# First pass over attention scores: masks added by VectorE with the maximum, or by TensorE products

## Chip, cores and metric

The kernel runs on one core of a Trainium2 chip. The metric is the device time of one execution in microseconds (us). Before the change it is 1712.83 us, the median of three runs (1712.34 to 1717.03).

## What is computed

Two layers on 2048 tokens of width 512, each an attention and a feed-forward part beside each other. The change lies in the attention of the second layer: 16 heads of width 32, causal, with a window of 1024 tokens back:

```python
q = rmsnorm(q, q_gamma); k = rmsnorm(k, k_gamma)
q = q * cos + rotate_half(q) * sin
k = k * cos + rotate_half(k) * sin
mask = (q_idx >= k_idx) & (q_idx - k_idx <= WINDOW)
scores = einsum('bhqd,bhkd->bhqk', q, k) / sqrt(HD)
scores = where(mask, scores, NEG)          # NEG = -1e30
attn = softmax(scores, axis=-1)
out = einsum('bhqk,bhkd->bhqd', attn, v)
```

The feed-forward part of the second layer chooses 256 of the tokens, and runs a small attention (heads of width 128) and a gated multilayer part on them alone.

## The kernel before, in words

**Two passes over the scores.** The kernel first makes all scores only to find the maximum of each query and head. A later stage makes them again, transposed, with the negated maxima added in a product, and takes the exponential. The first pass is `maxima` (L616). It works on one row of 128 queries at a time (i = 0 to 15), and in a row on groups g of four heads. A row sees the causal blocks of 128 keys back to the window, at most nine (NWB, L30); these are split in up to three chunks of at most four blocks. A chunk of one group is one *step*: a row has 4 steps in rows 0 to 3, 8 in rows 4 to 7, 12 in rows 8 to 15, 144 in all.

A step does the following. Four products of 32 contraction rows (one for each head, side by side in the array) write the scores into tile `pa` in PSUM, [128, 4, 512] (L633). Where a chunk holds the diagonal block (`last`) or, from row 8 on, the block at the window's edge (`edge`), four more products add a mask block: the identity times a mask of zeros and -1e30 in bf16 (L639, L641). No chunk holds both in its own blocks: where there is an edge there are three chunks, and 96 of the 144 steps have one mask. Then one VectorE reduction over all four heads writes the maxima of the chunk to `mx` (L645). `pa` has one buffer (pool `ps_a`, bufs=1, L719)[...]. At a row's end four small reductions (L649 to L653) turn the maxima into two bf16 parts of the negated maximum, four transposes (L658, tile `tn`) turn them, and ScalarE copies them to `negT`.

**What runs beside it.** The steps are cut up by a generator and spread by class `Steps` (L663): `some(below, weight)` adds a rate to a debt, and issues a step whenever the debt reaches one. Up to about row 7 the steps stand between the projections of the second layer (L965, 12 products of 512 columns for each token tile), the transposes (L110), and the routing that picks the 256 tokens. For each tile VectorE sums squares (L755), takes a reciprocal (L79), scales q and k (L758) and copies transposed k (L114); POOL rotates q and k (L763 to L773). Afterwards they stand between the feed-forward part's products: projections (L1042), its small attention (L1122, L1159), the output projection (L1175), gate and up (L1210, L1214), down (L1225). VectorE adds biases (L1047), masks and reduces scores (L1126, L1132) and multiplies (L1218) there. `late.rest()` (L1230) issues what is left. The second pass (L1285 on) begins with its first product at L1296, once `pa` has given its PSUM back.

**What sets the order.** Each engine works through its own queue in order. The source gives a priority, not the order itself: the tile framework schedules all instructions of the program when it is built, and may move an instruction past others of its engine. So the order in a queue can change where only an instruction's kind changes. Waits between engines, and of an engine on itself, are semaphores that the framework places.

Of the kernel before, what the change touches and what calls it, by code (L numbers as in the profile page):

```python
# [19 lines left out]
P = 128  # L20
# [18 lines left out]
def two_layer_kernel(ctx: ExitStack, tc: tile.TileContext, a: dict, out: bass.AP):  # L39
# [529 lines left out]
    G.tensor_copy(ident_b, ident)  # L569


    mask = const([P, 3, P], "mask", l1)
    maskT = const([P, 2, P], "maskT", l1)
    maskT_b = const([P, 2, P], "maskT_b", l1, BF16)
    mask_b = const([P, 3, P], "mask_b", l1, BF16)
    for m in (mask, maskT):
        G.memset(m, 0.0)
    for m, step, mult in (
        (mask[:, 0, :], 1, -1), (mask[:, 2, :], -1, 1), (maskT[:, 0, :], -1, 1), (maskT[:, 1, :], 1, -1)
    ):  # L580
        G.affine_select(
            out=m, in_=m, pattern=[[step, P]], compare_op=ALU.is_ge, fill=NEG, base=0,
            channel_multiplier=mult,
        )
    G.tensor_copy(mask_b, mask)
    G.tensor_copy(maskT_b, maskT)
    ones_b = const([P, P], "ones_b", l1, BF16)
    G.memset(ones_b, 1.0)
# [27 lines left out]
    def maxima(i, ps_a):  # L616


        nb = min(i + 1, NWB)
        kb0 = i + 1 - nb  # L620
        nch = -(-nb // 4)
        mx, nm, pn = mxs[i % 2], nms[i % 2], parts[i % 2]
        for g in range(NC):
            lo = 0
            for c in range(nch):
                w = nb // nch + (c < nb % nch)
                ks = slice((kb0 + lo) * P, (kb0 + lo + w) * P)
                edge = nb == NWB and c == 0
                last = c == nch - 1
                pS = ps_a.tile([P, 4, 4 * P], F32, tag="a", name=f"pa_{i}_{g}_{c}")  # L630
                for h in range(4):
                    r = slice(h * HD, (h + 1) * HD)
                    PE.matmul(  # L633
                        pS[:, h, : w * P], qT[r, g, i * P : (i + 1) * P], kT[r, g, ks],
                        start=True, stop=not (edge or last),
                    )
                for h in range(4):
                    if edge:
                        PE.matmul(pS[:, h, 0:P], ident_b, mask_b[:, 0, :], start=False, stop=True)  # L639
                    if last:  # L640
                        PE.matmul(  # L641
                            pS[:, h, (w - 1) * P : w * P], ident_b, mask_b[:, 2, :],
                            start=False, stop=True,
                        )
                V.tensor_reduce(mx[:, g, :, c], pS[:, :, : w * P], AX.X, ALU.max)  # L645
                yield
                lo += w

        V.tensor_reduce(nm[:, :, :, 0], mx[:, :, :, :nch], AX.X, ALU.max, negate=True)  # L649
        V.tensor_reduce(pn[:, :, :, 0], nm[:, :, :, 0:1], AX.X, ALU.max)  # L650
        V.tensor_reduce(nm[:, :, :, 1], pn[:, :, :, 0:1], AX.X, ALU.max, negate=True)
        with nc.allow_low_precision(reason="the low part of a split in two"):
            V.tensor_reduce(pn[:, :, :, 1], nm, AX.X, ALU.add)  # L653

        def turn(pool, tag):
            tn = pool.tile([P, NC, P], BF16, tag=tag, name=f"tn_{i}")
            for g in range(NC):
                PE.transpose(tn[:, g, :], pn[:, g].rearrange("p h d -> p (h d)"), ident_b)  # L658
            scopy(negT[:, :, i * P : (i + 1) * P], tn)

        yield turn
# [335 lines left out]
    with ExitStack() as p5:  # L997
# [110 lines left out]
        def attend(ch, q2T):  # L1108


            rep = NH2 // NKV2
            probs = []
            for j in range(2):
                n = (j + 1) * P
                nm = f"{ch}_{j}"
                pr = wk.tile([P, NHC, K2], F32, tag="pr", name=f"pr_{nm}")
                mx = wk.tile([P, 2, NHC], F32, tag="mx2", name=f"mx2_{nm}")
                for h0 in range(0, NHC, 2):
                    pS = ps.tile([P, 2, K2], F32, tag="mm", name=f"s2_{nm}_{h0}")
                    for hh in range(2):  # L1120
                        h = h0 + hh
                        PE.matmul(  # L1122
                            pS[:, hh, :n], q2T[:, h, j * P : (j + 1) * P],
                            k2T[:, (ch * NHC + h) // rep, 0:n], start=True, stop=True,
                        )
                    V.scalar_tensor_tensor(  # L1126
                        pr[:, h0 : h0 + 2, :n], pS[:, :, :n], 1.0 / math.sqrt(HD2),
                        mask[:, 2 - j : 3, :].rearrange("p b k -> p (b k)").unsqueeze(1)
                        .to_broadcast([P, 2, n]), ALU.mult, ALU.add,
                    )  # L1130
                late.some(weight=0.9 * (j + 1))
                V.tensor_reduce(mx[:, 0, :], pr[:, :, :n], AX.X, ALU.max, negate=True)  # L1132
                for hl in range(NHC):
                    S.activation(
                        pr[:, hl, :n], pr[:, hl, :n], AF.Exp, bias=mx[:, 0, hl : hl + 1],
                        accum_out=mx[:, 1, hl : hl + 1],
                    )
                V.reciprocal(mx[:, 1, :], mx[:, 1, :])
                for hl in range(NHC):
                    S.activation(  # L1140
                        pr[:, hl, :n], pr[:, hl, :n], AF.Copy, scale=mx[:, 1, hl : hl + 1]
                    )
                probs.append(pr)
            yield
            for j in range(2):
                nm = f"{ch}_{j}"
                pT = []
                for b in range(j + 1):
                    pT.append(wk.tile([P, NHC, P], F32, tag="pT", name=f"pT_{nm}_{b}"))
                    transpose4(  # L1150
                        ps, lambda c: probs[j][:, c, b * P : (b + 1) * P], pT[b],
                        f"trp_{nm}_{b}", scopy, tag="mm",
                    )
                late.some(weight=0.5 * (j + 1))
                po = ps.tile([P, NHC, P], F32, tag="mm", name=f"o2_{nm}")
                for h0 in range(0, NHC, rep):
                    kvh = (ch * NHC + h0) // rep
                    for b in range(j + 1):
                        PE.matmul(  # L1159
                            po[:, h0 : h0 + rep, :].rearrange("p h q -> p (h q)"),  # L1160
                            v2[:, b, kvh * HD2 : (kvh + 1) * HD2],
                            pT[b][:, h0 : h0 + rep, :].rearrange("p h q -> p (h q)"),
                            start=b == 0, stop=b == j,
                        )
                late.some(weight=0.9 * (j + 1))
                vcopy(oT[:, ch * NHC : (ch + 1) * NHC, j * P : (j + 1) * P], po)
            yield
# [336 lines left out]
```

## Time and profile before

| what | value |
|---|---|
| median of 3 runs | 1712.83 us |
| the profiled execution, its own time | 1715.47 us |
| its span | 1713.8 us |
| granted TensorE clock, mean | 0.994 |
| first and last score block of the first pass (start) | 747.8 and 1328.1 us |
| reductions L645 | 144, 252.9 us; 0.69, 1.22, 1.76, 2.29 us for one to four blocks |
| mask products L639 and L641 | 128 and 256, 12.7 and 25.6 us of records |

The page of the profile lists one execution. A group line gives source line, engine, operation, output and inputs with their shapes, and the number of instructions; then the busy time and the mean of one in ns; then the idle time of the engine in front of them, and what ended most of it. A record of a matrix product lasts longer than its share of the engine, since products overlap in the array: the spacing of starts tells what one costs. A product of fp32 data is two records. "PEld" is the loading of weights, which overlaps the products.

### The profile page before, as it was taken

Reading aid. Unit: us, or ns where it says so; the run is one execution under the profiler, and the core shown is the slowest. Engines: PE = TensorE matmul, PEld = TensorE weight load, DVE = VectorE, ACT = ScalarE, POOL = GpSimd, SP = SyncE. Lnnn points to the kernel's source line nnn. Section 1 sums busy time; section 2 is a strip of 40 time slices with the busy share of each in tenths; the row PEclk is TensorE's granted clock in tenths of the full one; section 3 lists DMA queues with packets and bytes.
Section 4 is the critical chain, followed back from the end, with each engine's and each line's share of the span. In section 5 each row is a group of like instructions: output and inputs, shape, how many; then the busy total and the mean of one; then the engine's idle time right before and its main releaser. Section 6 shows DMA issues by size and latency. Waiting matters only on the chain.

```text
span 1713.8 us, 20410 instructions
## 1 busy us (share of the span) xinstructions
PE 1657.4 (97%) x8114; PEld 743.6 (43%) x8114; DVE 982.5 (57%) x1256; ACT 588.2 (34%) x939; POOL 500.0 (29%) x398
## 2 busy tenths in 40 slices
PE   8999999999999999989999989899999999999999
PEld 3445444444444444444443434454564333333343
DVE  4754746345445543357566676675555477557565
ACT  3213333243253344221111110431100566447473
POOL 3230000000000200053574423330000677558584
PEclk9999999999999999999999999999899999999999
DMA  9411001120030431111010034112232300110101
GB/s 360 169 37 47 25 25 37 47 88 25 25 111 25 94 104 50 62 56 56 25 32 26 28 118 153 62 50 74 74 99 74 99 1 2 50 50 2 50 1 38
DMA packets 62384, 109.23 MB, mean 64 GB/s; under 512 B 12528, under 2 KB 14064, under 8 KB 61520
## 3 DMA queue, kind: packets, MB, share of 16 engines
q1 hardware_dynamic: 55856, 106.12, 18.7%
q0 software_dynamic: 1152, 1.21, 0.4%
q10 hardware_dynamic: 5280, 0.59, 0.3%
q8 instruction: 63, 1.03, 0.3%
q14 instruction: 33, 0.27, 0.1%
HBM read 86.24 MB, written 21.67 MB: 63 GB/s over the span
## 4 chain that ended last, share of the span: by engine, by line
PE 81%; DVE 10%; ACT 2%; DMA 2%; POOL 2%; issue 2%; SPq 0%; DVEq 0%; POOLq 0%; ACTq 0%
PE ea L494 6%; PE acc L478 6%; PE eg L492 6%; PE ps L1296 6%; PE pa L633 6%; PE p L965 6%; PE av L1370 5%; PE po L553 3%; PE pq L367 3%; PE po L1340 3%; PE gx L242 3%; DVE mx L645 3%; PE mg L1210 2%; PE pao L1175 2%; PE pm L1225 2%; PE po L555 2%
## 5 line engine op out<-in xcount | busy, mean ns | idle before, releaser
L645 DVE TENSOR_REDUCE mx<-pa 128x4 f32<-128x1536 f32 (+3 forms) x144 | 252.9, 1756 | 151.2 <-PE pa L641 72.2
L1403 POOL TENSOR_TENSOR acc<-acc,pt 128x1024 f32<-128x1024 f32 (+2 forms) x110 | 252.9, 2328 | 96.6 <-DVE acc L1403 43.4
L1330 ACT ACTIVATE pt<-ps 128x1024 f32<-128x1024 f32 (+3 forms) x208 | 181.4, 924 | 108.1 <-PE ps L1319 61.5
L1403 DVE TENSOR_TENSOR acc<-acc,pt 128x1024 f32<-128x1024 f32 (+1 forms) x80 | 144.4, 1832 | 103.9 <-POOL acc L1403 103.9
L633 PE MATMUL pa<-kT,qT 32*128 32x384 f32 (+3 forms) x1152 | 139.8, 541 | 19.8 <-DVE mx L645 16.1
L350 ACT ACTIVATE r_e<-eg 128x512 f32<-128x512 f32 x128 | 75.9, 594 | 201.6 <-PE eg L492 194.4
L1296 PE MATMUL ps<-qT,kT 32*128 32x512 f32 (+3 forms) x1152 | 139.9, 524 | 0.0
L352 DVE TENSOR_TENSOR h<-ea,r_e 128x512 f32<-128x512 f32 x128 | 87.2, 685 | 84.5 <-ACT r_e L351 83.5
L743 POOL TENSOR_TENSOR cosg<-cosg,gam 128x512 f32<-128x512 f32 x2 | 2.5, 1264 | 442.7 <-DVE gam L740 442.7
L492 PE MATMUL eg<-xl,rwgT 128*128 128x512 f32 x256 | 130.7, 592 | 0.0
L494 PE MATMUL ea<-xw,rw1T 128*128 128x512 f32 x256 | 130.7, 592 | 0.0
L478 PE MATMUL acc<-h,rw2T 128*128 128x512 f32 x256 | 129.2, 592 | 0.0
L965 PE MATMUL p<-w_qk,xnt 128*128 128x512 f32 x256 | 123.2, 604 | 2.3 <-DVE qk L758 2.3
L1370 PE MATMUL av<-pt,v 128*32 128x512 f32 (+3 forms) x1024 | 100.8, 482 | 0.0
L1296 PEld LDWEIGHTS ps<-qT,kT 32*128 32x128 f32 x1152 | 54.7, 183 | 94.7 <-issue 65.8
L633 PEld LDWEIGHTS pa<-kT,qT 32*128 32x128 f32 x1152 | 46.8, 185 | 103.3 <-DVE mx L645 64.9
L488 DVE TENSOR_TENSOR xw<-xw,xl 128x512 f32<-128x512 f32 x64 | 43.8, 685 | 83.5 <-DMA xw<-w_d 83.2
L351 ACT ACTIVATE r_e<-r_e 128x512 f32<-128x512 f32 x128 | 80.3, 629 | 5.7 <-ACT r_e L350 1.9
L478 PEld LDWEIGHTS acc<-h,rw2T 128*128 128x128 f32 x256 | 48.6, 190 | 61.3 <-issue 52.1
L492 PEld LDWEIGHTS eg<-xl,rwgT 128*128 128x128 f32 x256 | 48.6, 190 | 61.2 <-issue 61.0
L494 PEld LDWEIGHTS ea<-xw,rw1T 128*128 128x128 f32 x256 | 48.6, 190 | 61.2 <-issue 59.3
L288 PE MATMUL pk<-k_wT,xnT 128*128 128x512 f32 x128 | 61.3, 622 | 3.5 <-ACT xnT L117 3.5
(336 smaller groups left out, 2420.0 us busy)
## 6 DMA issues: line engine op xcount, KB each, us to landing
xw<-w_d SPq DMA_DIRECT2D x64, 256.0 KB, 3.2
x<-in_x SPq DMA_DIRECT2D x16, 256.0 KB, 4.7
res_d<-x SPq DMA_DIRECT2D x16, 256.0 KB, 2.1
xr<-res_d SPq DMA_DIRECT2D x16, 256.0 KB, 4.2
xn_d<-xn SPq DMA_DIRECT2D x16, 256.0 KB, 3.0
res_d<-xr SPq DMA_DIRECT2D x16, 256.0 KB, 3.1
xnq<-xn_d SPq DMA_DIRECT2D x16, 256.0 KB, 2.8
v_d<-vt SPq DMA_DIRECT2D x16, 256.0 KB, 2.0
```

The source lines that it names most:

```text
L351: S.activation(r, r, AF.Square)
L352: V.tensor_tensor(dst, pa, r, ALU.mult)
L478: PE.matmul(acc, rw2T[:, j, e, :], h, start=e == 0 and j == 0, stop=e == E - 1 and j == 1,)
L492: PE.matmul(pg, rwgT[:, e, hb], xl, start=True, stop=True)
L494: PE.matmul(pa, rw1T[:, e, hb], xw, start=True, stop=True)
L633: PE.matmul(pS[:, h, : w * P], qT[r, g, i * P : (i + 1) * P], kT[r, g, ks], start=True, stop=not (edge or last),)
L645: V.tensor_reduce(mx[:, g, :, c], pS[:, :, : w * P], AX.X, ALU.max)
L965: PE.matmul(pj, xnt[:, c, :], w, start=c == 0, stop=c == NC - 1)
L1296: PE.matmul(pS[h // 2][:, h % 2, t0 * P - q0 : (t1 + 1) * P - q0], kT[r, g, kb * P : (kb + 1) * P], qT[r, g, t0 * P : (t1 + 1) * P], start ...
L1330: S.activation(pT[:, :, :n], pS[hp][:, :, :n], AF.Exp)
L1370: PE.matmul(self.av[h * HD : (h + 1) * HD, t0 * P - o : (t1 + 1) * P - o], vs[kb // 4][:, kb % 4, hs], got[h // 2][:, h % 2, t0 * P - q0 : ...
L1403: eng.tensor_tensor(part, part, got[hp][:, :, : q1 - q0], ALU.add)
```

## The change

VectorE now adds the masks. `mask` gets five blocks in place of three (edge, three of zeros, diagonal), so that a slice of it fits every masked chunk, with the mask at its first or its last block. In a masked step the mask products are gone. The one reduction is replaced by four `tensor_tensor_reduce`, one for each head: each adds the mask slice to the scores in place in PSUM, and takes the maximum of the sums into one column of `mx`. In the built program each is two instructions, the operation and a read of its accumulator. Steps without a mask keep the reduction. The bf16 copy `mask_b` is gone, and the other user of `mask` (L1126) takes its slice from the new places.

```diff
--- before.py
+++ after.py
@@ -569,20 +569,18 @@
     G.tensor_copy(ident_b, ident)
 
 
-    mask = const([P, 3, P], "mask", l1)
+    mask = const([P, 5, P], "mask", l1)
     maskT = const([P, 2, P], "maskT", l1)
     maskT_b = const([P, 2, P], "maskT_b", l1, BF16)
-    mask_b = const([P, 3, P], "mask_b", l1, BF16)
     for m in (mask, maskT):
         G.memset(m, 0.0)
     for m, step, mult in (
-        (mask[:, 0, :], 1, -1), (mask[:, 2, :], -1, 1), (maskT[:, 0, :], -1, 1), (maskT[:, 1, :], 1, -1)
+        (mask[:, 0, :], 1, -1), (mask[:, 4, :], -1, 1), (maskT[:, 0, :], -1, 1), (maskT[:, 1, :], 1, -1)
     ):
         G.affine_select(
             out=m, in_=m, pattern=[[step, P]], compare_op=ALU.is_ge, fill=NEG, base=0,
             channel_multiplier=mult,
         )
-    G.tensor_copy(mask_b, mask)
     G.tensor_copy(maskT_b, maskT)
     ones_b = const([P, P], "ones_b", l1, BF16)
     G.memset(ones_b, 1.0)
@@ -632,17 +630,19 @@
                     r = slice(h * HD, (h + 1) * HD)
                     PE.matmul(
                         pS[:, h, : w * P], qT[r, g, i * P : (i + 1) * P], kT[r, g, ks],
-                        start=True, stop=not (edge or last),
+                        start=True, stop=True,
                     )
-                for h in range(4):
-                    if edge:
-                        PE.matmul(pS[:, h, 0:P], ident_b, mask_b[:, 0, :], start=False, stop=True)
-                    if last:
-                        PE.matmul(
-                            pS[:, h, (w - 1) * P : w * P], ident_b, mask_b[:, 2, :],
-                            start=False, stop=True,
+                if edge or last:
+
+                    m = mask[:, 0:w, :] if edge else mask[:, 5 - w : 5, :]
+                    m = m.rearrange("p b k -> p (b k)")
+                    for h in range(4):
+                        s = pS[:, h, : w * P]
+                        V.tensor_tensor_reduce(
+                            s, s, m, 1.0, LOW, ALU.add, ALU.max, accum_out=mx[:, g, h, c : c + 1]
                         )
-                V.tensor_reduce(mx[:, g, :, c], pS[:, :, : w * P], AX.X, ALU.max)
+                else:
+                    V.tensor_reduce(mx[:, g, :, c], pS[:, :, : w * P], AX.X, ALU.max)
                 yield
                 lo += w
 
@@ -1125,7 +1125,7 @@
                         )
                     V.scalar_tensor_tensor(
                         pr[:, h0 : h0 + 2, :n], pS[:, :, :n], 1.0 / math.sqrt(HD2),
-                        mask[:, 2 - j : 3, :].rearrange("p b k -> p (b k)").unsqueeze(1)
+                        mask[:, 4 - j : 5, :].rearrange("p b k -> p (b k)").unsqueeze(1)
                         .to_broadcast([P, 2, n]), ALU.mult, ALU.add,
                     )
                 late.some(weight=0.9 * (j + 1))
```

## The prediction

> **What bounds the kernel now.** The page first: its engine line says that TensorE is nearly full over the whole span, and group L645 that VectorE's maxima wait for TensorE, while TensorE's scores (L633) wait for the maxima.
>
> ```profile
> PE 1657.4 (97%) x8114; PEld 743.6 (43%) x8114; DVE 982.5 (57%) x1256; ACT 588.2 (34%) x939; POOL 500.0 (29%) x398
> ```
> ```profile
> L645 DVE TENSOR_REDUCE mx<-pa 128x4 f32<-128x1536 f32 (+3 forms) x144 | 252.9, 1756 | 151.2 <-PE pa L641 72.2
> L633 PE MATMUL pa<-kT,qT 32*128 32x384 f32 (+3 forms) x1152 | 139.8, 541 | 19.8 <-DVE mx L645 16.1
> ```
>
> Second the windows view, for the two halves of the stage where tile pa lives (query rows 0 to 7, then 8 to 15). Columns: PE, PEld, DVE, ACT, POOL busy.
>
> ```profile
> 748.00:957.00 209.00, 194.21 (x964) 86.55 (x960) 140.76 (x157) 38.70 (x75) 111.21 (x112) 0.99 0.12 32
> 957.00:1331.00 374.00, 353.47 (x1888) 184.01 (x1888) 232.72 (x237) 71.06 (x181) 69.89 (x89) 0.98 0.25 83
> ```
>
> PE is 94% busy in this stage (547.7 of 583), DVE 64%. TensorE is the bound, but thinly: third, the timeline of one exchange.
>
> ```profile
> 1243.77 0.93 PE L633 MATMUL pa<-kT,qT 32*128 32x384 f32 x8
> ...
> 1244.62 0.40 PE L639 MATMUL pa<-mask_b,ident_b 128*128 128x128 bf16 x4
> ...
> 1245.06 1.76 DVE L645 TENSOR_REDUCE mx<-pa 128x4 f32<-128x1536 f32 x1 [0.69 <-PE pa L639]
> 1245.08 1.95 PE L1210 MATMUL mg<-hT_b,wg 128*128 128x256 f32 x8
> ...
> 1246.96 0.93 PE L633 MATMUL pa<-kT,qT 32*128 32x384 f32 x8
> ...
> 1247.95 1.76 DVE L645 TENSOR_REDUCE mx<-pa 128x4 f32<-128x1536 f32 x1 [1.14 <-PE pa L633]
> ```
>
> There is one buffer of pa. Scores and masks fill it, the maximum empties it, and only then may the next scores start. So each step lasts as long as the longer of two things: TensorE's own work between two score blocks (here 0.85 scores, 0.24 masks, 0.22 for tn, 1.75 for mg), and the **loop** through pa. The loop of a masked step of three blocks is 1.29 from scores to maximum, 1.76 for it, and 0.05 or more back: 3.10, which is also the shortest spacing of such maxima (967.06 to 970.16 in the timeline). Unmasked: 0.99 + 1.76 + 0.05 = 2.80. The work in between is only a little longer.
>
> **The change, part by part.** Of 144 steps 96 are masked: 4 of one block, 8 of two, 76 of three, 8 of four.
>
> *Removed on PE*: 384 mask products. The timeline starts one every 0.056 us (four take 0.23), so 384 x 0.056 = about 22 us, all on the engine that bounds the stage.
>
> *Added on DVE*: 384 add-and-max instructions and 384 accumulator reads for 96 reductions. No row shows this instruction. The nearest, in the groups by form, read scores in PSUM with the mask in SBUF, and accumulate:
>
> ```profile
> L98 DVE SCALAR_TENSOR_TENSOR sj<-xn,wr 128x512 f32<-128x512 f32 x16 | 10.9, 684 | 0.1
> L1126 DVE SCALAR_TENSOR_TENSOR pr<-s,mask 128x512 f32<-128x512 f32 x8 | 5.3, 678 | 0.0
> L1126 DVE SCALAR_TENSOR_TENSOR pr<-s,mask 128x256 f32<-128x256 f32 x8 | 3.2, 419 | 4.7 <-PE s L1122 4.7
> L98 DVE DVE_READ_ACCUMULATOR sj<-xn,wr 128x1 f32 x16 | 1.3, 81 | 0.0
> ```
>
> On the line through 678 and 419 a head of three blocks takes 0.548, its accumulator read 0.08. In the built program every such instruction waits for the one before it on its own engine; rows that do so (L649 to L653) stand 0.04 apart. So 0.67 a head, 2.68 a step against 1.756: +0.92. For one, two and four blocks it is 1.61 against 0.69, 2.16 against 1.22, 3.19 against 2.29. Over 96 steps that is +88 us on DVE, to some 462 us of a stage of 600.
>
> Bounds. The low end: the page "VectorE: DVE Perf Modes" of the Trainium skill, section "Rules for kernel authors", tells one not to fuse chained operations for speed but to lower their count; here one becomes eight. Its errata section prices an operation from PSUM at 120 cycles plus one per element, at 0.96 GHz. By that four heads take 4 x 0.525 = 2.10 us; it gives no price for the accumulator read or the wait between, which the rows do: 2.68. My sum below is +11 us by the page and +20 by the rows; I take the rows. The high end, 0.8 a head: L332, another such operation from PSUM, takes 0.341 for 128 columns where the line gives 0.29, and writing back into PSUM may add as much again; sum +40. Two cycles per element I exclude, since both L98 (accumulating) and L645 take 1.04 ns per element.
>
> *The loop then*: a masked step of three blocks is 0.99 + 2.68 + 0.05 = 3.72 against 3.10: +0.62. The first add-and-max waits for all four heads' scores, so nothing of it starts sooner.
>
> *What moves.* Since the program is scheduled as it is built, the order of PE's instructions changes too. Comparing both built orders: masked steps get more other work behind them (4.4 us in place of 3.7 in many), which would cover 3.72; but the work of a row isn't more than before, so the end of a row has none. In rows 7 to 14 the last score block is followed directly by the next row's:
>
> ```
> before: pa_3_1  mu x3 mg x4  pa_3_2  mu x4   pa_0_0 (row 15)  tn  mg x4
> after:  pa_3_1  mu x4        pa_3_2          pa_0_0 (row 15)  tn  mg x4  mu x2
> ```
>
> There TensorE has 0.94 us of work in a loop of 3.72 (2.8 us idle); there are 13 such empty steps, and 9 more are short by over 0.3 us.
>
> I added up the larger of work and loop for all 144 steps in both orders. A 512-column f32 product counts two records of 0.43 us, 256 columns half, a 128-column transpose 2 x 0.11, and score blocks 0.43, 0.64, 0.85, 1.06 for one to four blocks; 0.09 for the load before a score block. In us:
>
> | rows | work before | larger, before | work after | larger, after |
> |---|---|---|---|---|
> | 0-3 | 71.5 | 71.5 | 73.0 | 73.0 |
> | 4-7 | 129.6 | 129.6 | 127.7 | 136.6 |
> | 8-11 | 177.6 | 178.8 | 163.5 | 187.5 |
> | 12-15 | 175.8 | 178.4 | 168.5 | 181.7 |
> | all | 554.5 | 558.3 | 532.7 | 578.8 |
>
> So 22 us of products go, TensorE's idle time in these loops grows from 4 to 46, and the balance is **+20.5 us**. With the old order and the new loop the sum is only +3. The trace has 580.2 from the first to the last score block, 22 above the sheet: other VectorE work in front of a maximum, a weight load at 1014 (5 us). I keep these 22 as they are.
>
> *Queued behind*: the changed DVE order puts 25 us of other operations (copies of kT, qk, act, biases) between the heads of masked steps, where they lengthen the loop. 22 of the 96 masked steps have no cover, so 25 x 22/96 = **+6 us**. Those operations themselves wait up to 2 us longer for heads in front of them; POOL's rotation waits for qk (62.9 us already), with a tile of time to spare.
>
> *At nothing*: the longer memset and the dropped cast on POOL (418 and 502 ns at 587 us) fall in a stage where POOL sits idle; uncovered they would gain a few tenths of a us. No DMA moves across another. From the first L1296 on, the orders of both programs are the same on every engine, so the last 383 us stay.
>
> Sum: 1715.5 (span 1713.8 and 1.7 around it) + 26 = 1742. The profiled execution is 2.6 above the median of 1712.8, so 1739.
>
> **Rivals.**
> - *Faster: the cover holds.* TensorE stays the bound in every step and the longer loop hides behind products, as 94% busy suggests; then only the 22 us go: 1691. Place: the 22 short steps at the ends of rows; they would have to find work. It decides at some 0.33 us a head: below that the sheet turns negative even with the new order, and no row is near. Chance 0.08.
> - *Balance.* Rows cheaper than the page and little interleaving: within 5 us (0.3%, about what a measurement can tell from none): 1713. Chance 0.08.
> - *VectorE becomes the bound.* In row 8, DVE has 8 x 2.68 + 4 x 1.76 of maxima, about 12 us of other work (3.6 for each of three token tiles: rr 1.22, its reciprocal 0.35, qk 2 x 0.69, kT 0.68; and the row's end), and must stand off for 12 x 1.0 us of scores: 52 us against 48 in the sheet. If the other work never fits, all 25 us land, or a head costs 0.8: +45 to +60, say 1765. For it: row 8 took 48.0 us before by the timeline, where its work in the sheet is 45.2. Against: much of that work fits while scores are made. Chance 0.27.
> - *Forecast*, 1722 to 1755: chance 0.57.
>
> The range leaves out the faster case, part of balance, and the upper end of the third: 1716 to 1778. Faster by over 0.3% 0.08, same 0.08, slower 0.84.
>
> **What would show it.** 384 add-and-max rows of 0.55 us for three blocks with 384 reads of 0.08, and DVE up by 88 us; 4 heads in 2.7 us; PE's waits for pa from 16 to over 40 us, most at ends of rows, two score blocks 3.7 apart with nothing between; the stage after unchanged in length. I am wrong if a head takes under 0.4 or over 0.8 us, if PE's idle time isn't at the ends of rows, or if the qk and POOL chain opens a wait of its own.

## The result, and the profile after

The changed kernel takes 1779.35 us (median of 4 runs, 1775.04 to 1779.95) against 1713.57 for the kernel before (4 runs): a ratio of 1.0375, 95% interval 1.0352 to 1.0398, **65.8 us slower**. The forecast was 1739, in a range that ended at 1778. The sign was right, the size less than half.

From the page of the changed kernel: the engines; the granted clock in 40 slices; the two groups that now take the place of the one maximum, and the scores.

```profile
PE 1669.2 (94%) x7730; PEld 738.2 (42%) x7730; DVE 1047.8 (59%) x1928; ACT 588.8 (33%) x939; POOL 499.6 (28%) x397
...
PEclk9999999999999999999998869899899899999999
...
L641 DVE CUSTOM_DVE_ANT_0 pa<-pa,mask 128x384 f32<-128x384 f32 (+3 forms) x384 | 212.5, 553 | 106.8 <-PE pa L631 97.8
...
L631 PE MATMUL pa<-kT,qT 32*128 32x384 f32 (+3 forms) x1152 | 148.9, 586 | 62.0 <-DVE mx L641 44.2
...
L645 DVE TENSOR_REDUCE mx<-pa 128x4 f32<-128x1536 f32 (+1 forms) x48 | 88.5, 1844 | 61.1 <-PE pa L631 60.9
```

Two things to see. TensorE now waits 62.0 us in front of score products (19.8 before). And although 384 mask products are gone, TensorE's busy time *grew*, by 11.8 us: its products became slower. The PEclk row says why: 8s and a 6 in the slices of the score stage, where before had a single 8:

```profile
PEclk9999999999999999999999999999899999999999
```

The timeline shows both in one place, the end of row 14 (start, us, engine):

```profile
1341.20 0.93 PE L631 MATMUL pa<-kT,qT 32*128 32x384 f32 x8
1344.85 0.93 PE L631 MATMUL pa<-kT,qT 32*128 32x384 f32 x8 [2.73 <-DVE mx L641]
1345.82 0.52 PE L658 MATMUL tn<-ident_b,parts 128*128 128x128 bf16 x4
1346.13 3.55 PE L1210 MATMUL mg<-hT_b,wg 128*128 128x256 f32 x8
```

Two score blocks stand 3.65 us apart with nothing between: the empty step of the prediction, called *bare* from here on. Then the same eight products mg that took 1.95 us in the kernel before take 3.55. The trace's clock record has half the clock from 1345.96 for 3.41 us. All stretches of half clock in this record last 3.41 us or a multiple of it, but for one that the end of the execution cuts short.

The windows view of one stretch (PE, PEld, DVE, ACT, POOL busy, then the granted clock) of the kernel after, and of the kernel before:

```profile
1021.00:1056.00 35.00, 20.03 (x84) 8.62 (x85) 21.22 (x58) 3.29 (x8) 0.00 (x0) 0.51 0.28 100
```
```profile
1021.00:1056.00 35.00, 35.00 (x176) 15.15 (x176) 22.47 (x20) 2.93 (x5) 16.58 (x24) 1.00 0.60 214
```

These are the ends of rows 7 and 8 in the changed kernel: 34 us on end at a clock of 0.51, TensorE busy for 57% of it.

**An account of the stage.** I cut each trace at the first score block and at the first product of the last stage (L1296 after), and measured in between: how long some TensorE record runs ("covered"), the rest ("idle"), how long the granted clock is at half, and TensorE's covered time in those stretches. A product takes about twice as long there (those of mg start 0.427 us apart, and 0.216 at full clock), so half of that covered time is my estimate of what the clock costs.

| kernel | time, us | ratio to before, 95% | stage | covered | idle | at half clock | covered at half |
|---|---|---|---|---|---|---|---|
| before | 1713.57 | 1 | 587.5 | 552.2 | 35.2 | 17.1 | 16.1 |
| after | 1779.35 | 1.0375 (1.0352 to 1.0398) | 648.8 | 561.6 | 87.2 | 116.1 | 83.8 |
| no_masks | 1701.98 | 0.9923 (0.9897 to 0.9949) | 574.3 | 539.7 | 34.6 | 34.1 | 31.2 |
| add_then_max | 1781.76 | 1.0380 (1.0355 to 1.0406) | 653.9 | 563.2 | 90.6 | 122.8 | 88.4 |
| both | 1795.89 | 1.0465 (1.0440 to 1.0490) | 667.3 | 579.7 | 87.6 | 109.2 | 80.0 |
| fill | 1757.36 | 1.0245 (1.0221 to 1.0270) | 631.4 | 567.2 | 64.2 | 61.4 | 45.7 |
| warm | 1785.41 | 1.0443 (1.0415 to 1.0470) | 653.7 | 566.2 | 87.5 | 92.2 | 69.1 |
| warm2 | 1762.81 | 1.0286 (1.0269 to 1.0303) | 635.1 | 562.8 | 72.3 | 64.9 | 55.9 |
| new_order | 1776.14 | 1.0366 (1.0349 to 1.0384) | 651.0 | 579.4 | 71.6 | 102.4 | 78.3 |
| old_order | 1753.17 | 1.0234 (1.0217 to 1.0251) | 629.9 | 556.7 | 73.2 | 68.3 | 61.0 |
| old_both | 1741.01 | 1.0162 (1.0140 to 1.0185) | 613.5 | 543.7 | 69.8 | 37.5 | 32.6 |
| old_halves | 1723.98 | 1.0060 (1.0042 to 1.0078) | 600.1 | 564.2 | 35.9 | 44.4 | 37.2 |
| halves | 1746.90 | 1.0192 (1.0175 to 1.0209) | 619.3 | 585.6 | 33.7 | 54.6 | 49.8 |
| before_halves | 1723.14 | 1.0055 (1.0028 to 1.0082) | 596.1 | 561.2 | 34.8 | 27.3 | 20.7 |

The times are medians, and each ratio is to executions of before that ran beside that kernel; the other columns come from the profiled execution, which in old_order stands 6 us above its median.

From before to after: mask products -22, idle +52, half clock (83.8 - 16.1) / 2 = +34; that makes +64 of a stage that grew by 61.3. The forecast had the first two (-22, and +48 of idle time) and not the third. Of the 87 us of idle time, 36 lie in 13 bare steps; before has one bare step, with 2.

### The profile page after: what moved, and what is told of

Same layout as the page of the kernel before. It is cut to its first block, busy times and chain, and to the rows that moved or that the text cites. A ratio compares the mean times of both kernels' runs of the same rounds, so it can differ in the third digit from the quotient of the medians.

```text
span 1778.2 us, 20386 instructions
## 1 busy us (share of the span) xinstructions
PE 1669.2 (94%) x7730; PEld 738.2 (42%) x7730; DVE 1047.8 (59%) x1928; ACT 588.8 (33%) x939; POOL 499.6 (28%) x397
## 4 chain that ended last, share of the span: by engine, by line
PE 79%; DVE 12%; POOL 3%; ACT 2%; DMA 2%; issue 2%; SPq 0%; DVEq 0%; POOLq 0%; ACTq 0%
PE pa L631 7%; PE acc L478 6%; PE eg L492 6%; PE ea L494 6%; PE ps L1296 6%; PE av L1370 5%; PE p L965 5%; PE po L553 3%; PE pq L367 3%; PE po L1340 3%; DVE pa L641 3%; PE gx L242 3%; PE mg L1210 2%; DVE mx L645 2%; PE mu L1214 2%
## 5 line engine op out<-in xcount | busy, mean ns | idle before, releaser
L641 DVE CUSTOM_DVE_ANT_0 pa<-pa,mask 128x384 f32<-128x384 f32 (+3 forms) x384 | 212.5, 553 | 106.8 <-PE pa L631 97.8
L631 PE MATMUL pa<-kT,qT 32*128 32x384 f32 (+3 forms) x1152 | 148.9, 586 | 62.0 <-DVE mx L641 44.2
L1296 PE MATMUL ps<-qT,kT 32*128 32x512 f32 (+3 forms) x1152 | 140.9, 534 | 2.5 <-DVE mx L641 2.5
L352 DVE TENSOR_TENSOR h<-ea,r_e 128x512 f32<-128x512 f32 x128 | 87.5, 685 | 86.3 <-ACT r_e L351 85.3
L965 PE MATMUL p<-w_qk,xnt 128*128 128x512 f32 x256 | 129.0, 628 | 3.6 <-DVE qk L758 3.5
L645 DVE TENSOR_REDUCE mx<-pa 128x4 f32<-128x1536 f32 (+1 forms) x48 | 88.5, 1844 | 61.1 <-PE pa L631 60.9
L631 PEld LDWEIGHTS pa<-kT,qT 32*128 32x128 f32 x1152 | 49.2, 199 | 161.5 <-DVE mx L641 77.9
L1296 PEld LDWEIGHTS ps<-qT,kT 32*128 32x128 f32 x1152 | 55.0, 185 | 96.8 <-issue 67.6
L494 PEld LDWEIGHTS ea<-xw,rw1T 128*128 128x128 f32 x256 | 48.6, 190 | 61.3 <-issue 58.6
L478 PEld LDWEIGHTS acc<-h,rw2T 128*128 128x128 f32 x256 | 48.5, 190 | 61.4 <-issue 52.7
```

The costliest lines, as they stand in the source:

```text
L352: V.tensor_tensor(dst, pa, r, ALU.mult)
L478: PE.matmul(acc, rw2T[:, j, e, :], h, start=e == 0 and j == 0, stop=e == E - 1 and j == 1,)
L494: PE.matmul(pa, rw1T[:, e, hb], xw, start=True, stop=True)
L631: PE.matmul(pS[:, h, : w * P], qT[r, g, i * P : (i + 1) * P], kT[r, g, ks], start=True, stop=True,)
L641: V.tensor_tensor_reduce(s, s, m, 1.0, LOW, ALU.add, ALU.max, accum_out=mx[:, g, h, c : c + 1])
L965: PE.matmul(pj, xnt[:, c, :], w, start=c == 0, stop=c == NC - 1)
```

## The experiments

The theories, as they stood when the runs were chosen. **Theory 1**: the built order leaves the ends of rows bare, the longer loop makes the wait there long, and beside its own length that wait makes the granted clock halve, so that later products cost more. **Theory 2**: the half clock is a by-product that costs nothing, because TensorE waits for VectorE in those stretches anyway. **Theory 3**: the order alone did it, not VectorE's instruction. **Theory 4** came later: VectorE's sheer length sets the pace.

**no_masks** (before, without any mask in the first pass):

```
-                        start=True, stop=not (edge or last),
+                        start=True, stop=True,
...
-                for h in range(4):
-                    if edge:
-                        PE.matmul(pS[:, h, 0:P], ident_b, mask_b[:, 0, :], start=False, stop=True)
...
```

> The kernel before without the mask products and without any addition on VectorE: the masks are left out of the first pass's maxima (the second pass keeps its own). Theory 1 (the changed kernel lost because the longer loop through pa leaves TensorE idle at the row ends, and because the granted clock then halves; the 22 us of mask products were a real gain): about 1690 us, 22 us below the kernel before, mean clock about 0.99, at most 20 us at half clock between the first score block and the last stage, TensorE idle in that stage about 35 us. Theory 2 (VectorE's queue sets the stage's end, the clock is a by-product): TensorE's 22 us were not on the path, so 1705 to 1715. Theory 3 (it is the built order of TensorE's work that lost the time): as theory 1, if the built order keeps its cover; it has 1 uncovered score step here, as before.

Measured: 1701.98, 0.9923 of before: faster than both kernels, but by 12 us and not 22. Its idle time is that of before, and it has 31.2 us covered at half clock against 16.1: (31.2 - 16.1) / 2 = 7.5 us of the 22 went into the clock. So the products that the change removes are real work, and at the same time they are cover: taking them away thins TensorE's load. Theory 1's 1690 is missed by 12 us and Theory 2's 1705 to 1715 by 3; it decides nothing between them by itself.

**add_then_max** (after, a masked step in two instructions of VectorE):

```
-                    for h in range(4):
-                        s = pS[:, h, : w * P]
-                        V.tensor_tensor_reduce(
-                            s, s, m, 1.0, LOW, ALU.add, ALU.max, accum_out=mx[:, g, h, c : c + 1]
-                        )
+                    m = mask[:, 0 if edge else 4, :].unsqueeze(1).to_broadcast([P, 4, P])
+                    V.tensor_tensor(pS[:, :, mc], pS[:, :, mc], m, ALU.add)
+                V.tensor_reduce(mx[:, g, :, c], pS[:, :, : w * P], AX.X, ALU.max)
```

> The changed kernel with a masked step made of two VectorE instructions instead of four and their reads: one in-place addition on the masked 128 columns of all four heads, then one maximum over the heads. Estimate of a three-block step: 0.7 us for the addition by the 512-element rows, 1.8 for the maximum, 2.5 in place of 2.65; VectorE gets no shorter than that. Theory 1: the gaps at the row ends stay (13 uncovered score steps in the built order, as in the changed kernel) and are 0.15 us shorter, the clock still halves there: 1765 to 1780 us, mean clock 0.96 to 0.975. Theory 2: VectorE is about 8 us shorter, so about 1771, whatever the clock does. It tells most about the instruction: if the instruction itself (its four reads, its waits) were at fault, this would come close to 1735.

Measured: 1781.76, the same loss, 2 us above the range of Theory 1. The page's rows of it:

```profile
L639 DVE TENSOR_REDUCE mx<-pa 128x4 f32<-128x1536 f32 (+3 forms) x144 | 252.9, 1756 | 61.8 <-PE pa L631 58.9
...
L638 DVE TENSOR_TENSOR pa<-pa,mask 128x512 f32<-128x512 f32 x96 | 67.0, 698 | 100.6 <-PE pa L631 100.2
```

0.698 + 1.756 make 2.45 us, near the 2.6 of four heads. Two instructions in place of eight win no time. The form of the instruction isn't the point; some 0.7 to 0.9 us more on VectorE in a masked step, and the order that is built for it, are.

**both** (mask products kept, VectorE's instruction on top, adding zeros):

```
+                if edge or last:
+                    z = mask[:, 1:2, :].to_broadcast([P, w, P])
...
+                        V.tensor_tensor_reduce(
+                            s, s, z, 1.0, LOW, ALU.add, ALU.max, accum_out=mx[:, g, h, c : c + 1]
+                        )
+                else:
+                    V.tensor_reduce(mx[:, g, :, c], pS[:, :, : w * P], AX.X, ALU.max)
```

> The kernel before with its mask products kept on TensorE, and the changed kernel's VectorE instruction on top, adding zeros: only VectorE's lengthening, without the relief of TensorE. Theory 1: the idle time and the half clock of the changed kernel, and 22 us of mask products back: about 1795 to 1810 us; the products lie inside the score steps, so the windows at the row ends are a little better covered and the half clock may be a little shorter. Theory 2 (VectorE is the bound): the products are hidden and it gives 1779 to 1788. Theory 3 (order): the built order has 13 uncovered steps, as in the changed kernel, so as theory 1.

Measured: 1795.89, 16.5 above the changed kernel. TensorE's covered time grew by 18.1 and its idle time stayed. Work added to TensorE is paid, as Theory 1 had it. Against Theory 2 this is weak evidence, though: the mask products stand between the scores and the maximum, so they lengthen the loop through `pa` as well, and a kernel that waits for that loop would pay for them too.

**fill** (after, 12 products that nobody reads at the ends of rows 7 to 15):

```
+FILL = {i: 12 for i in range(7, 16)}
...
+                    self.fill()
...
+                fl = self.pool.tile([P, D], F32, tag=self.tag, name=f"fill_{self.now}")
+                for _ in range(n):
+                    PE.matmul(
+                        fl, ones_b, ones_b.unsqueeze(1).to_broadcast([P, 4, P]),
+                        start=True, stop=True,
+                    )
```

> The changed kernel with 12 extra products of 128x512 (nobody reads them; each about 0.22 us at full clock, 2.6 us a row end) at the ends of rows 7 to 15, which stand in the built order between the last score blocks of the row: 23 us more TensorE work in all. Theory 1: they fill the gaps, so that fewer windows are under half covered; the half clock in the stage falls from 116 us to under 50, the mean clock rises to 0.98 or more, and the time falls although the work grew: 1745 to 1770 us. Theory 2 (the half clock costs nothing, VectorE's queue bounds): the time stays at 1775 to 1785, or grows by up to 23 us to about 1800 where the products don't fit a gap. Theory 3 (order): as theory 1 in part, since they are placed where the order is bare.

Measured: 1757.36. The page's rows of it, to be read beside those of the changed kernel:

```profile
PEclk9999999999999999999999869899999999999999
...
L632 PE MATMUL pa<-kT,qT 32*128 32x384 f32 (+3 forms) x1152 | 140.3, 558 | 39.6 <-DVE mx L642 26.7
```

With 23 us more work the kernel is 22 us *faster*. The products lie in the waits (idle 87.2 to 64.2), and the covered time at half clock falls from 83.8 to 45.7, worth 19 us. Theory 1 holds in the time, though 61 us are left at half clock where it had under 50; Theory 2 falls. But the scheduler was free to place these products, so the order was not held; hence the next two.

**warm** (after, its own order held; small products in the free columns of pa):

```
+                if n in FILL:
+                    FILLED[n] = [
+                        PE.matmul(
+                            pS[:, k % 4, w * P :], ones_b, ones_b, start=True, stop=True
+                        ).ins
+                        for k in range(FILL[n])
+                    ]
```

> The changed kernel in exactly its own built order, with 184 small products (ones by ones, 128x128 bf16, about 0.1 us each, 18 us in all, which nobody reads) put into 13 of the bare score steps, right behind the score products of the step, into the 128 columns of pa that a three-block step leaves unused: 8 to 16 of them a step, 0.9 to 1.7 us in a wait of 2.7. They shorten no wait and move nothing; only TensorE is busy for a larger part of those windows (2.6 of 3.65 us in place of 0.93). The three bare four-block steps of row 7 have no free columns and stay as they are. Theory 1: from row 8 on the clock stays full, half clock in the stage 116 to 60 us or less, mean clock 0.98 or more, and the time falls by the half-rate products, to 1748 to 1762 us, with the waits for VectorE as long as before. Theory 2 (half clock costs nothing): 1776 to 1785. Theory 3 (order): the order is that of the changed kernel, so the same time, 1776 to 1785.

Measured: 1785.41, just past the upper end of what Theories 2 and 3 had; but the trace shows that it doesn't test what it was made for. VectorE waited for the extra products, which write its own tile:

```profile
1342.72 1.07 PE L642 MATMUL pa<-ones_b 128*128 128x128 bf16 x16
1346.57 1.66 PE L634 MATMUL pa<-kT,qT 32*128 32x384 f32 x8 [2.78 <-DVE mx L653]
```

The wait of 2.78 us begins after the products instead of lying around them: they made each bare step 1.07 us longer and covered nothing. Inconclusive.

**warm2** (the same, with idle transposes into the tile that the next row's transposes overwrite):

```
             tn = pool.tile([P, NC, P], BF16, tag=tag, name=f"tn_{i}")
+            for n, k in FILL.get(i, {}).items():
+                FILLED[n] = [
+                    PE.transpose(tn[:, j % NC, :], ones_b, ident_b).ins for j in range(k)
+                ]
```

> As the run warm, mended: there VectorE waited for the extra products, since they wrote its own tile, and each of those steps grew by their 1.07 us. Here 216 idle transposes (ones, 128x128 bf16, about 0.1 us each, 22 us in all) write the tile of the next row's transposes, which nobody reads before those; they stand behind the score products of 13 bare steps (the three four-block steps of row 7 too) in exactly the changed kernel's order, and VectorE doesn't wait for them. Theory 1 (part of the loss is half clock, brought on by the idle row ends): half clock in the stage from 116 to under 60 us, TensorE idle from 87 to about 65 (the transposes lie in the waits), and the time falls to 1748 to 1762 us. Theory 2 (half clock costs nothing, TensorE waits for VectorE anyway): 1776 to 1785.

Measured: 1762.81, 16.5 below the changed kernel and 0.8 above the range of Theory 1 (65 us at half clock where it had under 60). The end of row 13 in the changed kernel, and then in warm2:

```profile
1295.06 0.93 PE L631 MATMUL pa<-kT,qT 32*128 32x384 f32 x8 [0.82 <-DVE mx L645]
1298.71 1.66 PE L631 MATMUL pa<-kT,qT 32*128 32x384 f32 x8 [2.72 <-DVE mx L641]
1300.30 0.61 PE L658 MATMUL tn<-ident_b,parts 128*128 128x128 bf16 x4
```
```profile
1283.03 0.93 PE L634 MATMUL pa<-kT,qT 32*128 32x384 f32 x8 [0.82 <-DVE mx L649]
1283.89 1.07 PE L663 MATMUL tn<-ident_b,ones_b 128*128 128x128 bf16 x16
1286.68 0.93 PE L634 MATMUL pa<-kT,qT 32*128 32x384 f32 x8 [1.72 <-DVE mx L645]
1287.65 0.40 PE L666 MATMUL tn<-ident_b,parts 128*128 128x128 bf16 x4
```

Both bare steps last 3.65 us; the transposes shorten no wait. But the scores behind them take 0.93 us and not 1.66. Over the stage the transposes add 14 us of work (216 at 0.067), idle time falls by 15, the covered time at half clock from 83.8 to 55.9, worth 14 us, and the stage is 13.7 shorter. In the traces TensorE's order (the transposes left out) and VectorE's are instruction by instruction those of the changed kernel, so this is the price of the clock, and it settles that part: not a by-product. The clock is still lost 13 times in the stage (15 in the changed kernel), since even with transposes some windows at bare steps are covered only for 0.48 to 0.50; but the stretches are shorter.

**old_order** and **new_order** take order and loop apart. Each holds TensorE's instructions to the other kernel's order (edges of issue order alone, no waits). old_order first, then new_order:

```
+    for x, y in zip(seq, seq[1:]):
+        tc.add_manual_dep(
+            y, x.name,
+            mybir.DependencyInfo(mybir.DependencyClass.NoSync, mybir.DependencyReason.DATA),
+            reason="order of before",
+        )
```

> The changed kernel with TensorE's built order held, instruction by instruction, to that of the kernel before (its mask products left out): the longer loop through pa alone, with the old cover. By the prediction's sheet the old order with the new loop is 3 to 5 us dearer at full clock than before, and one score step is bare instead of 13. Theory 1 (idle row ends and the half clock that they bring on; both need bare steps): 1713 to 1730 us, mean clock 0.985 or more, TensorE idle in the stage 45 to 55 us, under 60 us at half clock. Theory 2 (VectorE's queue sets the time): its work is the same as in the changed kernel, so 1770 to 1780. Theory 3 (it is the order alone): at or below before, 1695 to 1713, since the 22 us of mask products are gone.

> The other corner: the kernel before, mask products and all, with TensorE's built order held to that of the changed kernel; VectorE's work is that of before. Bare steps of the shorter loop: 13 of them wait about 1.8 us instead of 2.7, so 25 to 30 us more idle time than before; the products of a bare step cover about 1.24 of 3.1 us, 0.40, which is still below the half at which the changed kernel's windows lost the clock. Theory 1: 1745 to 1770 us with 60 to 110 us at half clock. Theory 2: VectorE is not longer, so within 10 us of before, 1713 to 1723. Theory 3: nearly all of the loss of the changed kernel, 1765 to 1800.

Measured: with the new order alone 1776.14, with the new loop alone 1753.17, with both (the changed kernel) 1779.35. Every theory missed old_order; Theory 3 alone has new_order in its range. The order alone, with VectorE's work unchanged and the mask products in place, gives +63: 36 us of idle time and (78.3 - 16.1) / 2 = 31 of half clock. "The order" means that of both engines here: VectorE's was not held, and in new_order's trace it stands much nearer to that of the changed kernel than to that of before. Which of the two queues does the harm isn't shown. In the new order the change itself is nearly free: it saves the 22 us of mask products and gives 16 of them back in idle time, 3 in half clock and 3 in the last stage. But the two effects don't add up: the order costs 63 without the longer loop and 26 with it, the loop 40 in the old order and 3 in the new. Either alone does most of the damage, and no share of the 66 belongs to one of them. The bare ends of rows, then, need no long loop to do harm: the timeline of new_order, at the same end of row 14, has a wait of 1.85 us in a loop of 3.11, and the clock is lost all the same (mg 2.57 in place of 1.95):

```profile
1342.60 0.93 PE L635 MATMUL pa<-kT,qT 32*128 32x384 f32 x8
...
1345.71 1.56 PE L635 MATMUL pa<-kT,qT 32*128 32x384 f32 x8 [1.85 <-DVE mx L649]
...
1348.03 2.57 PE L1214 MATMUL mg<-hT_b,wg 128*128 128x256 f32 x8
```

But the loop alone, in the good order, costs +40, where the prediction had +3. The waits view of old_order says where:

```profile
PE pa L631 <- DVE mx L641: 53.9, 50, 4.6
```

(This is the answer for the stage: engine and line that wait, for whom, us, times, longest.) Fifty waits of about 1.1 us on average have taken the place of the changed kernel's 19 of 2.3 (44.2 us). Part of it is VectorE's own order, which I had not held; its timeline:

```profile
1028.27 0.56 DVE L641 CUSTOM_DVE_ANT_0 pa<-pa,mask 128x384 f32<-128x384 f32 x1
1028.75 0.14 DVE L641 DVE_READ_ACCUMULATOR2_ANT mx<- 128x1 f32 x1
1028.75 1.22 DVE L763 TENSOR_TENSOR t<-qk,cosg 128x1024 f32<-128x1024 f32 x1
1029.88 0.56 DVE L641 CUSTOM_DVE_ANT_0 pa<-pa,mask 128x384 f32<-128x384 f32 x1
```

A step that was one instruction and is four can be parted: here 1.22 us of another tile's work stands between two heads, and pa isn't free until the last head is done.

**old_both** holds VectorE's order too, the four heads together:

```
+                        STEPS[-1].append(V.tensor_tensor_reduce(
...
+    for r in VORDER.split():
+        a, n = (int(x) for x in r[1:].split(":"))
+        for k in range(a, a + n):
+            seq += STEPS[k] if r[0] == "p" else [rest[k]]
```

> As old_order (1753), and VectorE's order held to that of before as well: the four heads of a masked step stand together, with no other operation between them. In old_order 48 of its longest idle gaps wait for such steps, whose four heads last 2.81 us on average (2.71 in the changed kernel, 2.64 as the prediction priced them), with copies of 0.69 and sums of 1.22 us among the heads. Theory 1a (the sheet's 3 us for the old order and the new loop were right but for those interleaved operations and the half clock that they bring on): idle in the stage 73 to 45 to 58 us, half clock 68 to under 45 us, 1715 to 1735 us. Theory 1b (the longer loop costs that much by itself: a step's work varies, and the sheet's means hide it): 1745 to 1756, idle above 65 us.

Measured: 1741.01, between the two expectations: the half clock (37.5 us) as Theory 1a had it, the idle time (70 us) as Theory 1b. VectorE's time from the first to the last instruction of the 144 steps falls by 30 us (358 to 328), the covered time at half clock nearly halves (61.0 to 32.6), and 12 us of time are won. Still +27 against before: the stage is 26 longer, of which the half clock is 8 and idle time 35, less 22 of products; 5 remain unassigned. By the sheet the idle time of these steps should have grown by about 25 (the 22 us that go, and the +3); the other 10 I can't assign to a place.

**old_halves**, **halves**, **before_halves** split the one buffer pa into two tiles of two heads, of the same size together. The first and the last hold TensorE's order to that of before:

```
-                pS = ps_a.tile([P, 4, 4 * P], F32, tag="a", name=f"pa_{i}_{g}_{c}")
+                pH = [
+                    ps_a.tile([P, 2, 4 * P], F32, tag=f"a{k}", name=f"pa{k}_{i}_{g}_{c}")
+                    for k in range(2)
+                ]
```

> The changed kernel in the order of before (as old_order, 1753), with pa in two tiles of two heads each[...]: TensorE may write heads 0 and 1 of the next step as soon as VectorE has read those two, not all four. VectorE's work is the same but for 48 more reductions, about 0.1 us each. Theory 1 as it stands now (the stage is a chain of 144 passes through one pa buffer: 475 of 587 us before, 549 of 649 in the changed kernel; what TensorE cannot put between is idle, and brings on the half clock): the loop that TensorE sees falls by about 1.3 us to 2.4 to 2.9 us, below the kernel before's 3.1; idle 73 to 40 us or less, half clock 68 to under 30 us, 1690 to 1715 us. Theory 4 (VectorE's own length, with its other operations queued among the heads, sets the pace, whatever the buffer): 1745 to 1758.

> The changed kernel with pa in two tiles of two heads each and no order held: the scheduler is free. Theory 1: the bare steps of its order remain but wait about 1.3 us less each, and the others find cover: 1715 to 1750 us, half clock in the stage under 80 us. Theory 4 (VectorE's length): 1770 to 1785. Theory 3 (the order alone): 1770 to 1780, if the order keeps its bare row ends.

> The kernel before in its own order, mask products and all, with pa in two tiles of two heads: what the split is worth without the change, so that old_halves can be read. The 144 maxima become 288 of half the length, about 0.1 us more for each pair (14 us on VectorE). Theory 1: idle of 35 us in the stage falls by 10 to 20 us, the little half clock (17 us) stays or goes, 1693 to 1706 us. Theory 4: VectorE is 14 us longer, 1712 to 1725.

Measured: 1723.98, 1746.90 and 1723.14. Theory 1 has halves within its range, old_halves 9 us above it, and before_halves 17 above it. The waits of old_halves for the masked heads, to be read beside old_order's 53.9:

```profile
PE pa L637 <- DVE mx L648: 8.8, 11, 2.9
```

VectorE's work is the same but for 48 more reductions, TensorE's order is the same, and the time is 29 us less (1753 to 1724). Part of the waiting has only moved, though: a score block that waits between its halves counts as covered, and the 144 blocks last 178 us in all, against 152 in old_order. Idle time falls by 37 us, of which 19 come back as covered time (counted at full clock); the half clock costs 12 less. halves is 32 us below the changed kernel (1779 to 1747), but it doesn't test the split alone: with two tiles the scheduler built another order, which has 2 bare steps in place of 13. Theory 1 had expected the bare steps to stay, so its hit there is in part luck. So in the old order VectorE's length is not the bound as such (Theory 4 falls there); what binds is that TensorE may not touch pa until VectorE is done with all of it. For the kernel before, whose waits were short, Theory 4 was the one to hold: the split brings nothing and costs 10 us. With the split and the old order the change is worth nothing either way (1723.98 against 1723.14), and neither beats the kernel before.

## Why the prediction came out as it did

- *22 us of mask products removed*: right as work (both pays 18 of it back). Net of what their absence does to the clock they were worth 12 us in no_masks.
- *A head of three blocks 0.67 us, a step 2.68*: right. The instruction takes 0.566 (0.548 estimated); its read 0.141 and not 0.08, but it overlaps the instruction's end, and heads follow each other at 0.66:

  ```profile
  1342.19 0.57 DVE L641 CUSTOM_DVE_ANT_0 pa<-pa,mask 128x384 f32<-128x384 f32 x1 [0.42 <-PE pa L631]
  1342.68 0.14 DVE L641 DVE_READ_ACCUMULATOR2_ANT mx<- 128x1 f32 x1
  1342.85 0.57 DVE L641 CUSTOM_DVE_ANT_0 pa<-pa,mask 128x384 f32<-128x384 f32 x1
  ```

  The page "VectorE: DVE Perf Modes" of the Trainium skill (its errata section on latency), against which I had weighed the rows, would give 0.525 for the instruction (its row is for results that go to SBUF; here they go back to PSUM): 7% short here. Two readings were slightly off, and change nothing: by its own rows a step of one block comes to 1.64 and not 1.61, and L98's row has one width only, so it gives no price for an element.
- *Loop 3.72 us*: measured 3.65.
- *13 bare steps, idle time +42 and +6*: right in place and size; measured +52, and 36 us idle in the 13 bare steps (13 x 2.8 forecast). What the sheet never priced is the new order with the old loop: new_order has the same 13 bare steps, and already 36 us more idle time than before.
- *The larger of work and loop, at durations from the trace of before*: this is **the step that failed**. Every product in the sheet, and the whole sum, has the duration of the full clock, which the trace of before nearly always showed. The clock is not even among the terms that the prediction put at nothing, and yet the idle time that it forecast is itself what takes the clock away. Measured in its place: products at half clock for 83.8 us of covered time in the stage, against 16.1 before, which is 34 us. The forecast of +26 with 34 added is +60; measured +65.8, of which 2.6 lie in the last stage.
- *The last 383 us stay*: nearly. Last stage 378.5 before, 381.1 after. It begins at 1397.0, and the clock is at half from 1397.16 for 10.2 us: the bare end of row 15 is paid for by products of the next stage.
- *"With the old order and the new loop the sum is only +3"*: wrong by 37 us in old_order and by 24 with VectorE's order held as well (old_both). The 12 between them are VectorE's order, operations among the heads included, mostly by way of the clock (half clock costs 22 us in old_order, 8 in old_both). Of the 24, 8 are half clock; 10 are idle time whose place stays open, and 5 are unassigned.
- *The rivals*: the time is nearest to "VectorE becomes the bound" (1765), but by another cause: old_halves leaves VectorE its work and takes back 29 of the 40 us that old_order had lost. "The cover holds" fell with the bare steps.

**The rule of the clock** as these traces show it. I cut each trace into the windows of 3.41 us in which the clock record changes. In the stage, all 15 times that the changed kernel lost the clock followed a window that TensorE's records covered for 0.20 to 0.47; no window covered for 0.59 or more was followed by a loss, and none lay between. The clock came back after windows covered for 0.98 or more; 0.6 or 0.8 was not enough. From 700 us to the end of the stage in all 14 traces, 119 of 130 losses came after a window covered for less than half, and 18 of 2357 full-clock windows that were followed by full clock were so thin; the clock came back after windows covered for 0.85 or more. That the window decides, not the gap, is my reading of these counts, and warm2's gain, with gaps as long but partly filled, supports it. The page "TensorE: Matmul & The Clock Gate" of the Trainium skill (section "HAM oscillation — how this bites in real kernels") warns of idle gaps over about 3.4 us; here a single gap of 1.81 in a window sufficed (loss at 1137.7 in the changed kernel; 1.85 in new_order's row 14), and only two gaps of the stage exceed 3.4 (4.6 and 4.85). The measurement decides: shorter gaps cost the clock too.

**Open**: 10 us of idle time in old_both; which of the two engines' orders costs what in new_order; why old_halves and halves keep 37 and 50 us covered at half clock. Not tried: a built order made for the longer loop, with work kept for the ends of rows.

## What to carry to other kernels

When a change makes an engine wait, price the wait twice: once for itself, and once for the products behind it, which in these traces ran at half clock when more than about half of a 3.41 us window had been empty; a sum from full-clock durations then comes out too low. Compare built orders before all else: here the old kernel in the new order lost nearly as much (63 us) as the changed one (66). And where one buffer ties two engines, look at how it is handed over: whole, the longer work on the reader cost 40 us in the old order; in two halves, it cost no more than the products that it replaced, though the halves themselves cost 10.

## What the hardware showed that I had not expected

- Useless products made the kernel faster: with 23 us of them it took 22 us less (fill), with 14 us 16.5 less (warm2).
- The clock came back only after a window that was full or nearly so (0.98 covered or more in the changed kernel), so that some thin stretches stayed at half clock for 20 and 34 us on end.
- The accumulator read of this instruction takes 0.141 us, against 0.081 for that of L98, and starts before the instruction's record ends.
